# Cross-attention in fp32 on one core: the V·Wo and A products of two steps made back to back, with their 64-row parts side by side

## The chip, the cores and the metric

One core of a Trainium2 chip runs the whole program. The time is microseconds of device time for one execution, and the median of several runs is what counts. The kernel before takes 275.19 us, the median of three runs (275.04 to 275.63).

## The reference

Sixteen batches, each with 256 query rows of 256 features (`x`) and 77 context rows of 192 features (`ctx_768`), eight heads, all in fp32:

```
Q = x @ Wq ; K = c @ Wk ; V = c @ Wv           (8 heads of 256)
score = Q K^T / sqrt(256), masked where mask == 0
attn  = softmax(score)
out   = (attn @ V) @ Wo + x
out   = layernorm(out) * gamma + beta
```

## The kernel before

**Folded weights.** The kernel multiplies weights together first. `gA` and `gB` hold Wk·Wq^T per head, for the first 128 and the last 64 of the 192 context features; `uA` and `uB` hold Wv·Wo in the same way. A batch then needs A (context times g, which meets `x` directly in the scores) and VW (context times u, which meets the softmax weights directly in the output). Each of the two is a sum over 192 features, made as a product over 128 rows (part A) and one over 64 rows (part B) that accumulate in the same PSUM bank. In part B two products run at a time, one on rows 0 to 63 of TensorE and one on rows 64 to 127.

**Steps.** After the weights are folded (the first 52 us of the trace) a loop over `b` from -1 to 14 takes one batch per step. Step `b` makes the scores of batch `b + 1` (two tiles of 128 query rows, `scores`, L289), then VW of batch `b + 1` (`prepare_vw`, tiles `pv`, two banks, L214 for part A and L225 for part B) and a quarter of A for the next group of four batches (`prepare_a`, tiles `pa`, four banks, L172 and L186), and then the output product of batch `b`. For batches 0 to 10 that is `seven(b)` (L422, tiles `pm` and `po`): seven products of 2x2 blocks after Strassen's manner in place of eight. They need sums of softmax blocks, `sums(b)`, four POOL instructions at L402 to L405, and differences of VW blocks, `differences(b)`, L385 on POOL. Batches 11 to 15 use `attend` (L354). A for a group is needed only when its first batch is scored; the quarters for group g are spread over the four steps before, and steps with `b + 1` of 12 and more make none.

**The order on every engine is the order of the program**: no scheduler moves anything, and each engine does its instructions one after the other. The order in one step is:

- TensorE (PE): scores of both tiles; `pv` part A, `pa` part A, `pv` part B, `pa` part B; `seven(b)`.
- VectorE (DVE): `shift` of both tiles (bias and row maximum, L304 and L311), a transpose of `vr` in some steps (L279), then for each tile the layernorm statistics of an older batch and the sum and reciprocal of its own softmax (L324, L326); one `normalise`; the two transposes of the softmax weights (`turn`, L342); transposes of `x` in every second pair of steps (L150); one more `normalise`; two `add_product` (L469).
- ScalarE (ACT): eight exponentials for each tile (L318), two small activations for the layernorm (L498, L499), six copies out of PSUM (two of `pv`, four of `pa`, L926), the copy of `pm` to `m` (L445).
- GpSimd (POOL): the softmax weights `p` (L332, four instructions), `differences(b + 1)`, then `add_seven(b)`: two additions within `m` and three into the output rows (L455), then `sums(b + 1)`.
- The DMA queue of SyncE (SP) loads `x` and stores finished rows.

So `sums(b + 1)` stands behind `add_seven(b)` on POOL, and `add_seven(b)` needs the finished `seven(b)`, through `m` and through `add_product` on DVE. `seven` uses the sums in the order s2, s3, s1, s4, from its second product on; POOL makes them in the order s1, s3, s2, s4.

**PSUM** has eight banks, given out in turn by one pool, `ps_mm`. A step takes four for the scores, two for `pv`, four for `pa`, one for `pm` and one for `po`. A product that opens a bank waits until the bank's use eight allocations before has been read.

Of the kernel before, what the change touches and what calls it, by code (L numbers as in the profile page):

```python
# [8 lines left out]
F32 = mybir.dt.float32  # L9
# [6 lines left out]
P = 128  # L16
# [3 lines left out]
GB = 4  # L20
# [5 lines left out]
def kernel(  # L26
# [13 lines left out]
    nc = tc.nc  # L40
    B, S, DI = x.shape
# [3 lines left out]
    NG = B // GB  # L45
# [23 lines left out]
    ps_mm = ctx.enter_context(tc.tile_pool(name="ps_mm", bufs=8, space=PSUM))  # L69
# [36 lines left out]
    def flat(ap):  # L106
        return ap.rearrange("p a b -> p (a b)")

    def half(i):
        return slice(i * LB, (i + 1) * LB)  # L110
# [18 lines left out]
    def in_two(name, shape, g):  # L129
        return pools[g % 2].tile(shape, F32, tag=f"{name}{g % 2}", name=f"{name}_{g}", bufs=1)  # L130
# [19 lines left out]
        nc.vector.transpose(cols, cols)  # L150


    def prepare_a(g, places, B_first=False):


        if 0 in places:
            a_of[g] = in_two("a", [P, 2, GB, H, S2], g)
        parts = [
            (2 * u + i, dc) for u in places for dc in range(2) for i in range(2)
        ]  # L160
        batches = slice(g * GB, (g + 1) * GB)
        banks = []

        def cols(dc, i):
            return slice((2 * i + dc) * BK, (2 * i + dc + 1) * BK)

        def part_A():
            if not B_first:
                banks.extend(ring_of(parts))
            for (h, dc), o in zip(parts, banks):  # L170
                for i in range(NM):
                    nc.tensor.matmul(  # L172
                        flat(o[i * BK : (i + 1) * BK]),
                        gA[:, h, cols(dc, i)],
                        flat(cA[:, batches, :]),
                        start=not B_first,
                        stop=B_first,
                    )

        def part_B():  # L180
            if B_first:
                banks.extend(ring_of(parts))
            for j in range(0, len(parts), 2):
                for i in range(NM):
                    for k, (h, dc) in enumerate(parts[j : j + 2]):
                        nc.tensor.matmul(  # L186
                            flat(banks[j + k][i * BK : (i + 1) * BK]),
                            gB[half(k), h // 2, cols(dc, i)],
                            flat(cB[half(k), batches, :]),
                            start=B_first,  # L190
                            stop=not B_first,
                        )

        def ring_of(parts):
            return [
                ps_mm.tile([P, GB, S2], F32, tag="mm", name=f"pa_{g}_{h}_{dc}") for h, dc in parts
            ]

        def copies():
            return [(a_of[g][:, dc, :, h, :], o) for (h, dc), o in zip(parts, banks)]  # L200

        return part_A, part_B, copies

    def prepare_vw(b):

        vw_of[b] = vwp.tile([P, 4, 2, P], F32, tag="vw", name=f"vw_{b}", bufs=3)
        parts = slice(0, 4) if b < NS else slice(1, 5)
        pv = []

        def part_A():  # L210
            for k in range(2):
                pv.append(ps_mm.tile([P, 2 * DI], F32, tag="mm", name=f"pv_{b}_{k}"))
                for i in range(NM):
                    nc.tensor.matmul(  # L214
                        pv[k][i * BK : (i + 1) * BK],
                        cA[:, b, k * BK : (k + 1) * BK],
                        uA[:, parts, :, i],
                        start=True,
                        stop=False,
                    )  # L220

        def part_B():
            for i in range(NM):
                for k in range(2):
                    nc.tensor.matmul(  # L225
                        pv[k][i * BK : (i + 1) * BK],
                        cB[half(k), b, k * BK : (k + 1) * BK],
                        uB[half(k), parts, :, i],
                        start=False,
                        stop=True,  # L230
                    )

        def copies():
            return [
                (vw_of[b][:, :, k, :], pv[k].rearrange("p (q d) -> p q d", q=4)) for k in range(2)
            ]

        return part_A, part_B, copies

    def prepare_last():  # L240
# [35 lines left out]
    def turn_last(n):  # L276

        blocks = flat(vr[:, 2 * n : 2 * n + 2])
        nc.vector.transpose(blocks, blocks)  # L279
# [41 lines left out]
    def weigh(t):  # L321
        e = e_of.pop(t)
        den = st.tile([P, H], F32, tag="den", name=f"den_{t}")
        nc.vector.tensor_reduce(den, e, AX.X, ALU.add)  # L324
        rden = st.tile([P, H], F32, tag="rden", name=f"rden_{t}")
        nc.vector.reciprocal(rden, den)  # L326
        p = p_ring[t % 2]
        e_mh = e.rearrange("p (m h) k -> p m h k", h=2)
        rden_mh = rden.rearrange("p (m h) -> p m h", h=2)
        for cols, keys in ((slice(2 * KM), slice(KM)), (slice(2 * KM, 2 * S2), slice(KM, None))):  # L330
            part = p[:, :, cols].rearrange("p m (h k) -> p m h k", h=2)
            nc.gpsimd.tensor_tensor(  # L332
                part,
                e_mh[:, :, :, keys],
                rden_mh.unsqueeze(3).to_broadcast(list(part.shape)),
                ALU.mult,
            )
# [226 lines left out]
    with tc.tile_pool(name="wonce", bufs=1) as wp:  # L564
# [304 lines left out]
        for u in (uA, uB):  # L869
            t2, _, b22, b11, b12 = (u[:, q].rearrange("p n i c -> p (n i c)") for q in range(5))  # L870
# [12 lines left out]
    pools[1] = vwp = late  # L883


    assert QT == 2
    last = NT - 1
    for b in range(-1, B - 1):
        old = range(max(b - 1, 0) * QT, b * QT)
        now = range(max(b, 0) * QT, (b + 1) * QT)  # L890
        new = range((b + 1) * QT, (b + 2) * QT)
        for t in new:
            scores(t)
        if b == B - 2:
            for t in old:
                finish(t)
            spread(old[0], old[-1] + 1)
            invert(old[0], old[-1] + 1, aside=old)
            for t in old:
                normalise(t, aside=True)  # L900
        for t in new:
            shift(t)
        for n in range(0, 2) if b < 0 else range(b + 2, min(b + 3, B // 2)):
            turn_last(n)
        g, n = (b + 1) // GB + 1, (b + 1) % GB
        work = [prepare_vw(b + 1)]
        if g < NG:
            work.append(prepare_a(g, (n,)))
        for part_A, _, _ in work:
            part_A()  # L910
        for _, part_B, _ in work:
            part_B()
        for i, t in enumerate(new):
            exponential(t)
            if old and b < B - 2:
                finish(old[i])
            weigh(t)
        if old and b < B - 2:
            spread(old[0], old[-1] + 1)
        if b < 0:  # L920
            bias_of(GB, B)
            for j in range(GT // 2, GT, 2):
                transpose_x(0, j)
        for _, _, copies in work:
            for dst, src in copies():
                nc.scalar.copy(dst, src)  # L926
        if b + 1 < NS:
            differences(b + 1)
        if b < NS:
            if now:  # L930
                seven(b)
            if old:
                invert(old[0], old[-1] + 1)
                normalise(old[0])
            for t in new:
                turn(t)
            if n >= NF - 2:
                for j in range((n - NF + 2) * GT // 2, (n - NF + 3) * GT // 2, 2):
                    transpose_x(g, j)
            if old:  # L940
                normalise(old[1])


            if n == NF - 1:
                load_x(g)
            elif n:
                load_xT(g, (n - 1) * GT // 2, n * GT // 2)
            if now:
                add_seven(b)
            if b + 1 < NS:  # L950
                sums(b + 1)
            continue
        for t in now:
            attend(t)
        if b < B - 2:
            invert(old[0], old[-1] + 1, aside=old[:1])
            normalise(old[0], aside=True)
            turn(new[0])
            normalise(old[1])
            turn(new[1])  # L960
            for t in now:
                add_product(t)
        else:
            turn(new[0])
            finish(now[0])
            spread(now[0], now[1])
            turn(new[1])
# [16 lines left out]
    rstd, _ = rstd_of.pop(t)  # L984
# [40 lines left out]
```

## Time and profile before

| | |
|---|---|
| median of three runs | 275.19 us |
| the profiled execution: its own time | 274.39 us |
| its span in the trace | 272.6 us |
| PE busy | 265.9 us |
| DVE busy | 211.7 us |
| POOL busy | 158.7 us |
| ACT busy | 136.2 us |
| granted TensorE clock over the span | 0.998 |
| step from 104.96 to 119.06 us | 14.10 us |
| the same for a step with `attend` (217.76 to 229.14 us) | 11.38 us |

Matmuls overlap, and their ends in the trace are modelled, so a busy PE isn't a PE at its peak; distances between starts say more than durations. The trace has two rows for each fp32 product, so that sixteen rows are eight products in the code. A step is timed here from its first score product to that of the next step. Idle time of an engine is listed with what ended it.

### The profile page before, as it was taken

How to read it: one execution, taken by the hardware profiler on the slowest of the kernel's cores; microseconds unless marked ns; L12 is line 12 of the kernel's file. 1: busy time of each engine (PE TensorE's matmuls, PEld its weight loads, DVE VectorE, ACT ScalarE, POOL GpSimd, SP SyncE). 2: the span in 40 equal slices, each digit the busy share in tenths (PEclk: the TensorE clock that was granted, in tenths of full speed). 3: DMA queues.
4: the chain of work that ended last, by engine and by line, in shares of the span. 5: the costliest groups of instructions: out<-in, count | busy, mean ns of one | idle time of the engine just before them, and what ended most of it. 6: DMA issues, size and time to landing. Idle time of an engine off the chain costs nothing.

```text
span 272.6 us, 13577 instructions
## 1 busy us (share of the span) xinstructions
PE 265.9 (98%) x6056; PEld 188.3 (69%) x6056; DVE 211.7 (78%) x414; ACT 136.2 (50%) x436; POOL 158.7 (58%) x217
## 2 busy tenths in 40 slices
PE   7999999999999999999999999999999999999992
PEld 6557587857595949494949595858687767584662
DVE  0555929589759898979798888878797978879875
ACT  3233324364828281818273746464645544827652
POOL 1000003719887878786878787777777537245754
PEclk9999999999999999999999999999999999999999
DMA  6999989920000403210231314101405060110102
GB/s 192 200 199 190 328 143 195 277 30 2 2 5 4 114 9 109 90 42 4 60 62 42 81 44 155 41 6 38 84 5 118 5 195 2 41 44 0 64 22 77
DMA packets 42458, 22.63 MB, mean 83 GB/s; under 512 B 23632, under 2 KB 41632, under 8 KB 42400
## 3 DMA queue, kind: packets, MB, share of 16 engines
q1 hardware_dynamic: 42400, 21.77, 34.1%
q8 instruction: 47, 0.77, 1.2%
q14 instruction: 11, 0.09, 0.1%
HBM read 17.57 MB, written 4.19 MB: 80 GB/s over the span
## 4 chain that ended last, share of the span: by engine, by line
PE 91%; DMA 5%; SPq 2%; DVE 1%; issue 0%; DVEq 0%
PE ps L289 25%; PE pa L172 11%; PE pv L214 10%; PE po L422 9%; PE pm L422 8%; PE po L354 7%; PE pv L225 6%; PE pa L186 5%; DMA wk_blk<-in_L_xattn_Wk_dram 5%; PE pu L723 3%; PE pr L248 2%; PE pgb L783 1%; PE pw L737 1%; PE pr L260 1%; SPq L582 1%; PE po L370 1%
## 5 line engine op out<-in xcount | busy, mean ns | idle before, releaser
L318 ACT ACTIVATE e<-s,top 128x77 f32<-128x77 f32 x256 | 67.1, 348 | 68.8 <-DVE top L311 68.8
L332 POOL TENSOR_TENSOR p<-e,rden 128x512 f32<-128x512 f32 x64 | 47.6, 765 | 43.3 <-DVE rden L326 28.1
L289 PE MATMUL ps<-a,xT 128*32 128x154 f32 x2048 | 70.0, 294 | 0.0
L289 PEld LDWEIGHTS ps<-a,xT 128*32 128x32 f32 x2048 | 66.1, 110 | 1.7 <-issue 0.8
L304 DVE TENSOR_TENSOR s<-ps,bias 128x308 f32<-128x308 f32 x64 | 30.1, 475 | 18.2 <-PE ps L289 18.2
L172 PE MATMUL pa<-cA,gA 128*32 128x308 f32 x512 | 36.0, 423 | 0.0
L172 PEld LDWEIGHTS pa<-cA,gA 128*32 128x32 f32 x512 | 16.3, 110 | 20.6 <-issue 7.9
L214 PE MATMUL pv<-uA,cA 128*32 128x512 f32 x256 | 30.4, 592 | 0.0
L455 POOL TENSOR_TENSOR xg<-xg,m 128x256 f32<-128x256 f32 x33 | 24.1, 732 | 10.6 <-DVE xg L469 8.8
L324 DVE TENSOR_REDUCE den<-e 128x8 f32<-128x616 f32 x32 | 24.8, 775 | 4.5 <-ACT e L318 4.4
L311 DVE TENSOR_REDUCE top<-s 128x8 f32<-128x616 f32 x32 | 25.4, 795 | 1.1
L342 DVE STREAM_TRANSPOSE pT<-p 128x640 f32<-128x640 f32 x32 | 25.2, 813 | 0.8 <-POOL p L332 0.8
L926 ACT COPY vw<-pv 128x512 f32<-128x512 f32 x32 | 17.1, 586 | 8.1 <-PE pv L225 8.1
L385 POOL TENSOR_TENSOR ts<-vw 128x768 f32<-128x768 f32 x11 | 20.2, 1839 | 0.0
L538 DVE SCALAR_TENSOR_TENSOR xg<-xg,rstd,bet 128x256 f32<-128x256 f32 x24 | 18.8, 782 | 1.8
L186 PE MATMUL pa<-cB,gB 64*32 64x308 f32 x512 | 19.8, 420 | 0.0
L600 POOL COPY cRA<-cA 128x208 f32<-128x208 f32 x1 | 0.4, 357 | 29.7 <-DVE cA L599 29.7
L186 PEld LDWEIGHTS pa<-cB,gB 64*32 64x32 f32 x512 | 9.5, 107 | 11.6 <-issue 8.1
L225 PE MATMUL pv<-uB,cB 64*32 64x512 f32 x256 | 17.4, 601 | 0.0
L354 PE MATMUL po<-vw,pT 128*32 128x256 f32 x288 | 17.3, 380 | 0.0
L926 ACT COPY a<-pa 128x308 f32<-128x308 f32 x48 | 16.8, 454 | 0.0
L469 DVE TENSOR_TENSOR xg<-po,xg 128x256 f32<-128x256 f32 x31 | 11.7, 414 | 5.2 <-PE po L422 4.6
(117 smaller groups left out, 400.5 us busy)
## 6 DMA issues: line engine op xcount, KB each, us to landing
xT<-in_x_dram SPq DMA_DIRECT2D x32, 128.0 KB, 4.4
xg<-in_x_dram SPq DMA_DIRECT2D x4, 1024.0 KB, 6.4
out_dram<-xg SPq DMA_DIRECT2D x11, 256.0 KB, 2.6
wo<-in_L_xattn_Wo_dram SPq DMA_DIRECT2D x4, 512.0 KB, 6.3
wq_blk<-in_L_xattn_Wq_dram SPq DMA_DIRECT2D x12, 128.0 KB, 4.5
wvT<-in_L_xattn_Wv_dram SPq DMA_DIRECT2D x16, 96.0 KB, 4.1
out_dram<-xg SPq DMA_DIRECT2D x10, 128.0 KB, 1.7
wk_blk<-in_L_xattn_Wk_dram SPq DMA_DIRECT2D x12, 96.0 KB, 4.4
```

The source lines that it names most:

```text
L172: nc.tensor.matmul(flat(o[i * BK : (i + 1) * BK]), gA[:, h, cols(dc, i)], flat(cA[:, batches, :]), start=not B_first, stop=B_first,)
L186: nc.tensor.matmul(flat(banks[j + k][i * BK : (i + 1) * BK]), gB[half(k), h // 2, cols(dc, i)], flat(cB[half(k), batches, :]), start=B_fir ...
L214: nc.tensor.matmul(pv[k][i * BK : (i + 1) * BK], cA[:, b, k * BK : (k + 1) * BK], uA[:, parts, :, i], start=True, stop=False,)
L225: nc.tensor.matmul(pv[k][i * BK : (i + 1) * BK], cB[half(k), b, k * BK : (k + 1) * BK], uB[half(k), parts, :, i], start=False, stop=True,)
L289: nc.tensor.matmul(ps[m // 2][i * BK : (i + 1) * BK, m % 2 * 2 * S2 : (m % 2 + 1) * 2 * S2], xT_of[g][:, j * NM + m, dc], flat(a_of[g][:, ...
L304: nc.vector.tensor_tensor(s[:, a * H // 2 : (a + 1) * H // 2], ps[a][:, : H // 2 * S2].rearrange("p (h k) -> p h k", k=S2), bias[:, b, :]. ...
L311: nc.vector.tensor_reduce(top, s, AX.X, ALU.max, negate=True)
L318: nc.scalar.activation(e[:, h], s[:, h], AF.Exp, bias=top[:, h : h + 1])
L332: nc.gpsimd.tensor_tensor(part, e_mh[:, :, :, keys], rden_mh.unsqueeze(3).to_broadcast(list(part.shape)), ALU.mult,)
L354: nc.tensor.matmul(po[i * BK : (i + 1) * BK], pT[:, n, i], vw_of[b][:, 2 - n // 2 * 2 : 4 - n // 2 * 2, n % 2, :] if n < NF else vr[:, b, ...
L422: nc.tensor.matmul(out[i * BK : (i + 1) * BK], weight[:, i], moving, start=(n == 0), stop=(n == len(terms) - 1),)
L926: nc.scalar.copy(dst, src)
```

## The change

`prepare_vw` and `prepare_a` can now make their part B first: the 64-row products open the banks (`start`) and the 128-row products close them (`stop`). The order of parts within a product is decided by `rest_first`.

The loop makes the work for batches `b + 1` and `b + 2` in one step, when `b + 1` is even and below 14, and none in the step after. The pairs of batches are (0, 1), (2, 3) up to (12, 13): seven pairs. Batches 14 and 15 are made each in its own step, as before. In a step with a pair, PE does part A and part B of batch `b + 1`, then part B and part A of batch `b + 2`, and then `seven(b)`. The step after it does scores and `seven` alone.

On ACT, the six copies for batch `b + 1` stand after the exponentials of the step's first tile and ahead of those of the second; the six for batch `b + 2` stand where the copies stood before. The order of instructions on DVE, POOL and the DMA queue is as it was.

```diff
-    def prepare_a(g, places, B_first=False):
+    def prepare_a(g, places, rest_first=False):
...
-                        start=not B_first,
-                        stop=B_first,
+                        start=not rest_first,
+                        stop=rest_first,
...
-    def prepare_vw(b):
+    def prepare_vw(b, rest_first=False):
...
-        pv = []
+        pv = [ps_mm.tile([P, 2 * DI], F32, tag="mm", name=f"pv_{b}_{k}") for k in range(2)]
...
-                        start=True,
-                        stop=False,
+                        start=not rest_first,
+                        stop=rest_first,
...
-                        start=False,
-                        stop=True,
+                        start=rest_first,
+                        stop=not rest_first,
...
+    def work_of(b, rest_first=False):
+        g, n = b // GB + 1, b % GB
+        work = [prepare_vw(b, rest_first)]
+        if g < NG:
+            work.append(prepare_a(g, (n,), rest_first))
+        return work
+
+    def copy_out(work):
+        for _, _, copies in work:
+            for dst, src in copies():
+                nc.scalar.copy(dst, src)
+
...
-        work = [prepare_vw(b + 1)]
-        if g < NG:
-            work.append(prepare_a(g, (n,)))
-        for part_A, _, _ in work:
+        works = work_of(b + 1) if b + 1 >= B - 2 or n % 2 == 0 else []
+        for part_A, _, _ in works:
             part_A()
-        for _, part_B, _ in work:
+        for _, part_B, _ in works:
             part_B()
         for i, t in enumerate(new):
             exponential(t)
             if old and b < B - 2:
                 finish(old[i])
             weigh(t)
+            if i == 0 and works and b + 1 < B - 2:
+                copy_out(works)
+                works = work_of(b + 2, rest_first=True)
+                for _, part_B, _ in works:
+                    part_B()
+                for part_A, _, _ in works:
+                    part_A()
...
-        for _, _, copies in work:
-            for dst, src in copies():
-                nc.scalar.copy(dst, src)
+        copy_out(works)
```

More of the change, by code (lines that the diff above doesn't have):

```diff
@@ L167, in part_A @@
         def part_A():
-            if not B_first:
+            if not rest_first:
                 banks.extend(ring_of(parts))
@@ L175, in part_A @@
                         flat(cA[:, batches, :]),
-                        start=not B_first,
-                        stop=B_first,
+                        start=not rest_first,
+                        stop=rest_first,
                     )
         def part_B():
-            if B_first:
+            if rest_first:
                 banks.extend(ring_of(parts))
@@ L189, in part_B @@
                             flat(cB[half(k), batches, :]),
-                            start=B_first,
-                            stop=not B_first,
+                            start=rest_first,
+                            stop=not rest_first,
                         )
@@ L202, in prepare_a @@
         return part_A, part_B, copies
-    def prepare_vw(b):
+    def prepare_vw(b, rest_first=False):
         vw_of[b] = vwp.tile([P, 4, 2, P], F32, tag="vw", name=f"vw_{b}", bufs=3)
         parts = slice(0, 4) if b < NS else slice(1, 5)
-        pv = []
+        pv = [ps_mm.tile([P, 2 * DI], F32, tag="mm", name=f"pv_{b}_{k}") for k in range(2)]
         def part_A():
             for k in range(2):
-                pv.append(ps_mm.tile([P, 2 * DI], F32, tag="mm", name=f"pv_{b}_{k}"))
                 for i in range(NM):
@@ L228, in part_B @@
                         uB[half(k), parts, :, i],
-                        start=False,
-                        stop=True,
+                        start=rest_first,
+                        stop=not rest_first,
                     )
```

## The prediction

> **What bounds the kernel now.** I read the page's busy times first, then the chain of waits, then the order in time of each engine in a step from the middle.
>
> The page, busy time by engine:
>
> ```profile
> PE 265.9 (98%) x6056; PEld 188.3 (69%) x6056; DVE 211.7 (78%) x414; ACT 136.2 (50%) x436; POOL 158.7 (58%) x217
> ```
>
> The chain of waits between 100 and 131 us (start, length, what), one full step:
>
> ```profile
> 105.15 4.19 PE ps L289 x128
> 109.33 1.72 PE pv L214 x16
> 111.05 2.07 PE pa L172 x32
> 113.12 1.02 PE pv L225 x16
> 114.14 1.04 PE pa L186 x32
> 115.18 1.89 PE pm L422 x64
> 117.06 2.18 PE po L422 x80
> 119.25 4.19 PE ps L289 x128
> ```
>
> Nothing but PE stands in it, so PE never waits for another engine inside a step. Everything else has slack only as long as it is ready when PE gets there, and that is what a new order on PE can break. The order in time of that step, for those who feed PE:
>
> ```profile
> 112.91 3.08 POOL L332 TENSOR_TENSOR p<-e,rden 128x512 f32<-128x512 f32 x4 [1.83 <-ACT e L318]
> 115.11 0.65 PE L422 MATMUL pm<-vw,pT 128*32 128x128 f32 x16
> 115.95 1.84 POOL L385 TENSOR_TENSOR ts<-vw 128x768 f32<-128x768 f32 x1
> 117.18 0.59 ACT L445 COPY m<-pm 128x512 f32<-128x512 f32 x1 [0.59 <-PE pm L422]
> 119.06 4.37 PE L289 MATMUL ps<-a,xT 128*32 128x154 f32 x128
> 119.82 2.35 POOL L455 TENSOR_TENSOR xg<-xg,m 128x256 f32<-128x256 f32 x3 [0.83 <-DVE xg L469]
> 122.13 0.73 POOL L402 TENSOR_TENSOR ss<-pT 128x256 f32<-128x256 f32 x1
> 123.62 0.73 POOL L404 TENSOR_TENSOR ss<-pT,ss 128x256 f32<-128x256 f32 x1
> ```
>
> Here `seven` starts at 115.11 and the next scores at 119.06, 3.95 us later. The sum s2 (L404), which the second product of the next `seven` needs, ends at 124.35, which is 5.29 us after those scores began. Before, ten microseconds of other products (4.19 + 1.72 + 2.07 + 1.02 + 1.04) lie between the start of the scores and that `seven`.
>
> **The change, part by part.** S is the start of a step's first score product.
>
> *Fewer changes between 128-row and 64-row products (gain).* In the chain, products over 128 rows take equal time for equal columns: the 80 rows of `po`, 128 columns each, take 2.18 us, so the 64 of `pm` should take 64/80 of it, 1.74; they take 1.89, 0.15 more, and they come right behind 64-row products. The 32 rows of `pa` part B, 308 columns each, take 1.04, so 16 rows of 512 columns should take 0.86; `pv` part B takes 1.02, 0.16 more, right behind 128-row products. A pair of changes costs 0.31. Before, two steps have two pairs; after, one. Seven times 0.31 is 2.2 us gained. The bounds: nothing, if B behind B' (marked ' is the work for batch b + 2) costs a change too, and 7 x 0.35, if the pipeline restarts a little more often than I see. I take 2.1. The Trainium skill, "TensorEngine Tiling (Array Packing)", Key Properties, says that a change of tiling mode drains TensorE, while another tile of the same mode doesn't; that rule alone would let the change be faster, by the sum just given.
>
> *Part B' must find its banks free.* Counting banks, the four banks of `pa'` are those of `pv` and the first two of `pa`, so B' waits for the copies on ACT, which the change puts behind the first tile's exponentials. By the middle step, exponentials of the first tile run from S + 3.75 to 5.85, `pv` part B ends so that the copies start at S + 9.27, take 1.07 for `pv` (to 10.34) and 1.40 for all `pa` (the second of these ends at about 10.95). PE would get to the first pair of `pa'` at 10.9 and to the second at 11.4. No wait if ACT is on time. Where the short step before leaves DVE behind, it isn't: I work out below that this happens once or twice, for 0.4 in all (bounds 0 and 2).
>
> *PE of the long step.* Up to the end of part B it is as before, S + 10.0. B' adds 0.86 + 1.04, a change 0.15, A' 1.72 + 2.07; `seven(b)` starts at T = S + 15.85, the next scores at T + 3.95.
>
> *The second tile's exponentials* now stand behind six copies on ACT: they start at S + 11.75 in place of 5.85 and end at 13.85. Row sum and reciprocal on DVE (0.76 + 0.20) give 14.95, the weights on POOL (1.54) 16.6, `differences` (1.84) 18.45. The two additions within `m` come next and their input `m` is ready at T + 2.66, that is S + 18.5. So POOL is just in time, and the delay of 5.9 us costs nothing as long as A' covers it; with a dearer chain each tenth is a tenth on the sums. Behind the wait on DVE stand `normalise`, `turn`, the transposes of x in every second pair (1.26) and `add_product`. With the transposes DVE gets to `add_product` at S + 20.25, 0.2 after `seven` is done; without, it is on time.
>
> *The short step (loss).* There scores run straight into `seven(b + 1)`. PE gets to its second product at 4.19 + 0.46 = 4.65 us behind the start of scores. s2 stands behind `add_seven(b)` on POOL, which starts as before with `add_product` after `seven(b)`, and so still ends 5.29 us behind the start of scores. The wait is 0.64, plus the time from POOL's end to PE's start. No row of before shows PE waiting for POOL; the nearest are POOL to DVE (`p` to its transpose, 0.03) and PE to ACT (0.3); I take 0.15. So PE stands idle 0.8 us in steps 2, 4, 6, 8, 10, and 0.2 more in the three behind transposes: 4.6 us. The other inputs, `differences`, VW and the softmax transposes, are there earlier. s4, needed 1.9 us behind s2, ends 0.8 behind it.
>
> *The first short step (b = 0)* has no `add_seven` ahead, but its sums wait for the late exponentials. These lines are step -1 in the order of time:
>
> ```profile
> 61.76 1.08 ACT L926 COPY vw<-pv 128x512 f32<-128x512 f32 x2 [1.38 <-PE pv L225]
> 64.16 1.74 POOL L560 TENSOR_TENSOR bias<-bias,nan 128x924 f32<-128x924 f32 x1
> 65.85 1.83 POOL L385 TENSOR_TENSOR ts<-vw 128x768 f32<-128x768 f32 x1
> 69.14 0.74 POOL L404 TENSOR_TENSOR ss<-pT,ss 128x256 f32<-128x256 f32 x1
> ```
>
> Copies until 64.12, exponentials until 66.2, row sum and reciprocal until 67.25, then the bias of the later batches on DVE (0.70 + 1.12, to 69.1), the small POOL steps and the bias on POOL as in these lines (63.58 to 65.90 there; 69.5 to 71.85 now), `differences` next, and s2 ends 4.03 behind the start of `differences`, at 75.85. PE: part B ends where step 0 began, 62.64; less one change 62.5; with B', A' and a change 68.35; scores to 72.55; the first product to 73.0. The wait ends at 76.0: 3.0 us lost (2.4 to 3.4).
>
> *No cost:* the moved copies and exponentials are as many as before. No DMA, DVE or POOL instruction is moved. DVE (12 us of work in a step) falls 3 to 4 us behind in a short step of 9 us and makes it up in the long one, 20 us; this is what delays the first exponentials of a long step from S + 5.85 to about S + 8.6, with both transposes of x and of `vr` (1.26 more) to about 9.9. The copies then start 0.6 late, and B', with 0.2 to 0.4 to spare, waits for the rest: this is the 0.4, which takes two such places. The last pair, batches 12 and 13, is followed by `attend`, which takes no sums: its transposes are ready at about S + 13.7 and needed at S + 17.8.
>
> *Sum:* -2.1 + 0.4 + 4.6 + 3.0 = +5.9 us. Against the profiled execution (274.39, span 272.6) that is 280.3, and against the median, 0.8 above it, 281.1.
>
> The first wait, 3.0 us, is the longest that PE would have behind the first score product; the granted clock of before is 1.00 in the steps that I read up to 251.89 us, and no row there tells what such a wait does to it. The Trainium skill, "TensorE: Matmul & The Clock Gate", Why this matters for your kernels, asks for no PE gap above some 3 us, or the clock falls to half; at that rule's window of about 3.4 us at half speed, an estimate from that page, the sum would be some 1.7 us higher.
>
> **Rivals.**
>
> *The sums are in time (faster, other side).* If s2 ended 0.8 us sooner relative to `seven`, the five waits would go and only the changes count. It decides at 5.29 against 4.65 us. POOL has no idle time between `add_seven` and L404, and 0.83 ahead of it is the wait for PE and DVE, which the change doesn't shorten: against. With the first step's wait gone as well it would be 275.2 - 2.1 = 273.1. Chance 0.06.
>
> *Banks bind.* If ACT comes 1 us later than I think in most long steps, because DVE starts the shift late, B' waits each time, and so does the chain behind the second exponentials: 0.6 on PE in each of six long steps, 3.6, and as much again at the sums if POOL, which is just in time, slips with it; less the 0.4 that I have, 287.9 at most and 284.5 with the first alone. DVE's 78% speaks for it, the 0.4 to 3.4 us of slack against. Chance 0.12.
>
> *The change doesn't do what it says:* the 0.31 stays, because opening a bank or the neighbouring B costs as much. Then 283.2. The 64-row `pa` behind `pv` shows no such cost. Chance 0.10.
>
> *Half the waits,* if POOL is faster with DVE held elsewhere: 278.3. Chance 0.10; the forecast itself has 0.62.
>
> **How the numbers follow.** 0.2% is about what a measurement of this kernel can tell from no change (0.55 us). Only the first rival ends below: faster 0.06, within 0.2% 0.02 (the case of half the waits, at its end, cancels the gain), slower 0.92. The forecast's own bounds are 2.4 + 5 x 0.6 - 2.4 = +3.0 and 3.4 + 5 x 1.2 + 1 - 1.5 = +8.9; from 278.2 to 284.1. This leaves out the first rival and the end of the second.
>
> **What would show it.** The chain of waits has POOL `ss` in it (L403 in the new numbering), and PE waits some 0.8 to 1.0 us for it in five short steps and about 3 us in the first; short steps take about 9 us and long ones 19.8, against 2 x 14.10. The long step has one pair of changes. The granted clock stays at 1.00. I am wrong if PE doesn't wait at all in short steps, if the waits lie in the long steps at `pa'`, or if the pair of changes isn't cheaper.

## The result, and the profile after

The changed kernel takes 282.04 us, the median of five runs (281.67 to 282.60); the kernel before took 275.19 beside it. The ratio is 1.0248, with an interval of 1.0224 to 1.0272: slower by 2.5%, 0.9 us above the forecast and inside its range. The execution shown took 282.13 us, its span is 280.3, 7.7 more than the 272.6 of before (by the medians the difference is 6.85; the execution of before that the profile shows was 0.8 us quicker than its median). Line numbers from here on are those of the changed kernel: from `prepare_vw` to `add_product` they are one lower than before (scores L288, `pm` and `po` L421, sums L401 to L404).

The busy time by engine, and further down the page the chain that ended last:

```profile
PE 266.5 (95%) x6056; PEld 190.6 (68%) x6056; DVE 209.9 (75%) x414; ACT 134.0 (48%) x436; POOL 157.6 (56%) x217
...
PE 58%; DVE 13%; ACT 10%; POOL 10%; DMA 5%; SPq 2%; issue 2%; DVEq 0%; POOLq 0%; ACTq 0%
```

PE has the same work to do (6056 rows, 266.5 us of modelled busy time against 265.9) in a longer span. Before, 91% of the chain was PE; now a third of it is DVE, ACT and POOL. What PE waits for now and didn't before (us in total, times, the longest):

```profile
PE pm L421 <- POOL ss L403: 4.8, 6, 2.1
PE po L353 <- DVE pT L341: 1.4, 1, 1.4
```

The first row is the sum s2, six times. The second, transposed softmax weights in the last step, is in no sum of the forecast. The chain through one wait for s2:

```profile
95.32 1.75 PE pm L421 x64
97.07 2.23 PE po L421 x80
99.29 0.02 issue
99.32 0.44 DVE xg L468
99.75 0.07 issue
99.82 0.74 POOL xg L454
...
101.44 0.73 POOL xg L454
102.18 0.69 POOL ss L401
102.87 0.70 POOL ss L402
103.57 0.07 issue
103.64 0.74 POOL ss L403
104.38 0.04 issue
104.42 1.52 PE pm L421 x48
105.94 2.18 PE po L421 x80
```

From the end of `seven` at 99.3 us the chain leaves PE for `add_product`, three additions and three sums, and comes back at 104.42. On PE the next scores lie beside that and end sooner:

```profile
99.07 4.37 PE L288 MATMUL ps<-a,xT 128*32 128x154 f32 x128
103.25 0.62 PE L421 MATMUL pm<-vw,pT 128*32 128x128 f32 x16
104.42 0.65 PE L421 MATMUL pm<-vw,ss 128*32 128x128 f32 x16 [0.55 <-POOL ss L403]
```

The first product at 103.25 and the second at 104.42 are 1.17 us apart where 0.43 to 0.46 is usual, so the wait costs 0.73 (0.55 by the row, the rest while the weights are loaded behind it).

The time by step, as stretches from one step's first scores to the next's (length; busy us and rows of PE, PEld (TensorE's weight loads), DVE, ACT, POOL; granted clock; DMA share; GB/s):

```profile
53.00:68.88 15.88, 15.88 (x322) 8.94 (x324) 8.26 (x16) 8.79 (x28) 2.83 (x4) 1.00 0.25 35
68.88:79.28 10.40, 8.33 (x276) 8.05 (x272) 9.26 (x17) 5.15 (x19) 8.97 (x13) 1.00 0.01 3
79.28:99.07 19.79, 19.79 (x473) 12.84 (x469) 13.39 (x27) 9.82 (x31) 14.56 (x19) 1.00 0.02 4
99.07:107.94 8.87, 8.32 (x281) 8.03 (x276) 7.31 (x17) 4.69 (x19) 5.97 (x8) 1.00 0.40 92
107.94:128.16 20.22, 20.22 (x473) 12.92 (x467) 17.23 (x33) 10.01 (x33) 15.50 (x21) 1.00 0.24 68
...
223.19:280.30 57.11, 49.94 (x1088) 33.25 (x1079) 47.74 (x106) 28.38 (x96) 29.23 (x43) 0.99 0.17 53
```

The last stretch, from the scores of batch 12 on, in the kernel before:

```profile
217.76:272.60 54.84, 50.04 (x1088) 32.86 (x1080) 43.38 (x98) 28.68 (x96) 26.73 (x39) 0.99 0.18 55
```

PE has as much to do in it, but DVE brings 4.4 us of work more into it (47.74 against 43.38). The 7.7 us of the span, part by part:

| part | before | after | difference |
|---|---|---|---|
| up to the first scores (loads) | 52.47 | 53.00 | +0.53 |
| steps -1 and 0 | 24.29 | 26.28 | +1.99 |
| steps 1 to 10, five pairs | 141.00 | 143.91 | +2.91 |
| from the scores of batch 12 | 54.84 | 57.11 | +2.27 |

A short step takes 8.11 us where nothing waits (two of the experiments below show it), so the first wait costs 10.40 - 8.11 = 2.29 and the other five 0.76 each. A long step takes 19.79 where no bank waits, so a pair without waits takes 27.90 against 28.20: 0.30 is saved.

### The profile page after: what moved, and what is told of

It is laid out like the page before. It is cut to its first block, busy times and chain, and to the rows that moved or that the text cites. A ratio compares the mean times of both kernels' runs of the same rounds, so it can differ in the third digit from the quotient of the medians.

```text
span 280.3 us, 13587 instructions
## 1 busy us (share of the span) xinstructions
PE 266.5 (95%) x6056; PEld 190.6 (68%) x6056; DVE 209.9 (75%) x414; ACT 134.0 (48%) x436; POOL 157.6 (56%) x217
## 4 chain that ended last, share of the span: by engine, by line
PE 58%; DVE 13%; ACT 10%; POOL 10%; DMA 5%; SPq 2%; issue 2%; DVEq 0%; POOLq 0%; ACTq 0%
PE ps L288 10%; PE pa L172 10%; ACT e L317 8%; PE po L421 8%; PE pv L213 7%; PE pm L421 6%; PE pa L186 5%; DMA wk_blk<-in_L_xattn_Wk_dram 5%; PE pv L224 4%; POOL xg L454 3%; PE pu L722 3%; DVE pT L341 2%; PE pr L247 2%; DVE xg L468 2%; DVE den L323 2%
## 5 line engine op out<-in xcount | busy, mean ns | idle before, releaser
L288 PE MATMUL ps<-a,xT 128*32 128x154 f32 x2048 | 69.9, 294 | 0.0
L288 PEld LDWEIGHTS ps<-a,xT 128*32 128x32 f32 x2048 | 66.3, 110 | 1.4 <-issue 0.3
L303 DVE TENSOR_TENSOR s<-ps,bias 128x308 f32<-128x308 f32 x64 | 28.4, 469 | 7.9 <-PE ps L288 7.9
L895 ACT COPY a<-pa 128x308 f32<-128x308 f32 x48 | 17.4, 438 | 0.6
L213 PEld LDWEIGHTS pv<-uA,cA 128*32 128x32 f32 x256 | 7.6, 110 | 13.4 <-issue 12.5
```

Of the source, the lines that this page charges most:

```text
L213: nc.tensor.matmul(pv[k][i * BK : (i + 1) * BK], cA[:, b, k * BK : (k + 1) * BK], uA[:, parts, :, i], start=not rest_first, stop=rest_first,)
L288: nc.tensor.matmul(ps[m // 2][i * BK : (i + 1) * BK, m % 2 * 2 * S2 : (m % 2 + 1) * 2 * S2], xT_of[g][:, j * NM + m, dc], flat(a_of[g][:, ...
L303: nc.vector.tensor_tensor(s[:, a * H // 2 : (a + 1) * H // 2], ps[a][:, : H // 2 * S2].rearrange("p (h k) -> p h k", k=S2), bias[:, b, :]. ...
```

## The experiments

The theory at first: the loss is PE's waits for s2, the first of them made by the bias work on POOL. The rivals: the dearer part is at the end, where DVE or the missing cover of a product delays `attend`; and the price of the changes between 128-row and 64-row products isn't what I took.

**The last pair undone.** Only the last pair, batches 12 and 13, goes back to two single steps.

```diff
-        works = work_of(b + 1) if b + 1 >= B - 2 or n % 2 == 0 else []
+        works = work_of(b + 1) if b + 1 >= B - 4 or n % 2 == 0 else []
...
-            if i == 0 and works and b + 1 < B - 2:
+            if i == 0 and works and b + 1 < B - 4:
```

> The changed kernel with batches 12 and 13 made each in its own step again; the pairs (0, 1) to (10, 11) stay. In the changed kernel the stretch from the scores of batch 12 to the end takes 57.1 us against 54.8 before, 2.3 us more where I had forecast 0.3 less. Theory A, the last pair's own short step keeps DVE and ACT late until the end: with full steps of 11.4 us for 9.7 us of DVE work the lag of some 4.5 us is worked off by the last step, the stretch takes about 54.8, the time is 279.8 (279.4 to 280.2) and no wait for the transposed softmax is left. Theory B, the lag handed on by the short step before (batch 11) is enough: the stretch stays near 57 us and the time at 282.0 or, without the gain of one pair, 282.3.

It took 281.18 us (280.77 to 283.44), ratio 1.0249 (1.0204 to 1.0293). The wait for `pT` is gone, and the stretch from the scores of batch 12 takes 56.17 us (223.03 to 279.2): 0.94 of the 2.27 are gone, 1.33 stay. (The times alone wouldn't show it: the ratio is that of the kernel after, 1.0248.) So the last pair explains less than half of what the end lost, and each of the two theories named there has its half.

**Two pairs undone.** The same with `B - 6` in both conditions: pairs only up to (8, 9).

> The changed kernel with the pairs (0, 1) to (8, 9) alone; batches 10 to 13 are made each in its own step. The run with batches 12 and 13 apart took only half of the 2.3 us off the end (56.2 us from the scores of batch 12 on, before 54.8): DVE came 3.9 us late out of the short step ahead and was still 1.6 us late in the last step. If that lag is the cause, two more full steps work it off: the stretch from the scores of batch 12 takes 54.8, and the time is 2.3 + 0.5 us under the changed kernel, 279.3 (278.8 to 279.7). If the end is long for another reason: 281 or more.

280.54 us (279.69 to 282.51), ratio 1.0212 (1.0178 to 1.0246), 1.2 us above what the theory gave; the profiled execution lost 1.65 us in step 0 to the clock, of which more below. The stretch from the scores of batch 12:

```profile
225.89:280.70 54.81, 50.03 (x1088) 32.84 (x1079) 44.76 (x101) 28.57 (x96) 26.71 (x39) 0.99 0.18 55
```

That is the 54.84 of before: with two ordinary steps of 14.10 us between the last short step and the end, nothing is lost there. The reason is DVE's lag. ACT's first exponentials of batch 12, in the kernel before and after:

```profile
221.51 4.20 ACT L318 ACTIVATE e<-s,top 128x77 f32<-128x77 f32 x16 [5.04 <-DVE top L311]
...
230.78 2.11 ACT L317 ACTIVATE e<-s,top 128x77 f32<-128x77 f32 x8 [7.62 <-DVE top L310]
```

The scores began at 217.76 and 223.19, and ACT stood idle for DVE's row maximum. The time from a step's first scores to its first exponential, in us (3.75 in the steps before, without lag 4.1 in the last one, where layernorm work stands ahead):

| batch scored | 12 | 13 | 14 | 15 |
|---|---|---|---|---|
| before | 3.75 | 3.69 | 3.68 | 4.09 |
| after | 7.59 | 4.87 | 6.64 | 6.93 |
| last pair undone | 7.60 | 6.50 | 5.39 | 5.68 |
| two pairs undone | 4.24 | 3.68 | 3.69 | 4.08 |

A short step of 8.87 us is shorter than DVE's work (11.9 to 12.5 us in the steps of 14.10 before), and what DVE owes then is paid off at about 1.1 us for each step of 11.38 us up to batch 14 (7.60, 6.50, 5.39). The rate isn't PE's 11.38 less DVE's 9.7 us of work: DVE and ACT wait for each other in turn (row maximum, exponentials, row sum), and that chain takes 10.27 us for a batch (first exponentials at 230.63, 240.90 and 251.17 in the run with the last pair undone). Into batch 15, where layernorm work stands ahead of the exponentials, it takes 11.67 (to 262.84), and nothing more is paid off. In the kernel after, the steps of batches 12 and 13 make 13.95 + 8.50 = 22.45 us instead of 2 x 11.38, so they don't pay it off either. At batch 15 the exponentials are 2.84 us late (6.93 - 4.09), and the last step is 2.57 longer (23.28 us from its first scores to the end, before 20.71); the pair saves 0.31 of it elsewhere. The chain of the kernel after at that place:

```profile
252.28 4.11 ACT e L317 x16
256.41 0.81 DVE den L323
257.45 0.71 DVE pT L341
...
262.95 1.09 ACT xg L531 x2
264.04 4.01 ACT e L317 x16
268.07 0.81 DVE den L323
269.10 0.71 DVE pT L341
270.16 0.44 DVE bn L476
```

There is no PE in it. From the scores of batch 12 to the end the chain is on DVE and ACT, but for some 2.3 us on POOL.

**The sums ahead of `add_seven` on POOL.**

```diff
-            if now:
-                add_seven(b)
             if b + 1 < NS:
                 sums(b + 1)
+            if now:
+                add_seven(b)
```

> The changed kernel with the four POOL instructions of sums(b + 1) placed ahead of the five of add_seven(b). My theory: PE's 0.74 us waits in the five short steps hang on add_seven standing ahead of the sums; they go (3.7 us), the 2.1 us wait in step 0 stays, since no add_seven stands there. As each short step is then 0.74 us shorter and DVE has as much to do, DVE comes later into the long steps, and part is given back as waits for PSUM banks there, 1.5 to 2.5 us: 280 to 281. If nothing is given back, 278.3. Rival, another input of seven is as late as the sums: 282.0, and the trace names that input.

282.13 us (281.42 to 284.49), ratio 1.0282 (1.0233 to 1.0330): no gain, a miss. PE's waits show where it went:

```profile
PE po L353 <- DVE pT L341: 2.1, 1, 2.1
PE pm L421 <- POOL ss L403: 2.1, 1, 2.1
...
PE pa L172 <- DVE xg L468: 1.3, 2, 0.7
```

Five of the six waits for s2 are gone and the short steps take 8.11 us. But then DVE has still less time in them, and long steps take 21.11, 20.37, 20.87 and 20.13 where 19.79 is free of waits. In the two longest `pa` waits for a bank that `add_product` reads, and in all four weight loads of B' wait for ACT's copies (0.28 to 0.41 us). The five pairs lose 1.84 instead of 2.91, and the end (57.9) 0.8 more than after. So the wait for s2 is real, but under it lies DVE, and most of what POOL gives back is lost again behind it.

The same edit in the kernel before, as a control:

> The kernel before with the four POOL instructions of sums(b + 1) ahead of the five of add_seven(b), as a control for the order on POOL: PE never waits for either there, so 275.0, no change (within 0.4 us).

274.92 us (274.18 to 275.79), ratio 0.9999 (0.9985 to 1.0012). With the cover of ten microseconds of products, the order of POOL is free.

**The price of a change of rows, from both sides.** In the changed kernel the pair is made as A, B, A', B', so that B' no longer stands beside B:

```diff
-                works = work_of(b + 2, rest_first=True)
-                for _, part_B, _ in works:
-                    part_B()
+                works = work_of(b + 2)
                 for part_A, _, _ in works:
                     part_A()
+                for _, part_B, _ in works:
+                    part_B()
```

> The changed kernel with part A of the second batch of a pair made ahead of its part B, so that the order on PE is A, B, A', B', seven: two more changes between 128-row and 64-row products for each of the seven pairs, nothing else. My theory, a pair of changes costs 0.31 us: 7 x 0.31 = 2.2 us, 284.2 (283.7 to 284.5), if each lands on the path. Rival, the order of parts is worth nothing: 282.0.

283.30 us (282.62 to 284.74), ratio 1.0316 (1.0280 to 1.0352), 1.3 above the changed kernel by the medians and 1.9 by the ratios, where the theory gave 2.2. A long step without a bank wait takes 20.08 against 19.79, so 0.29; where a bank wait of up to 0.4 lay in it, it takes 20.21 against 20.22: the later B' has its bank free. That gives back 0.5 in two steps, and another 0.27 and 0.26 come back from shorter waits in step 0 and at the end. And in the kernel before, `pv` and `pa` each do A and then B:

```diff
-        for part_A, _, _ in work:
+        for part_A, part_B, _ in work:
             part_A()
-        for _, part_B, _ in work:
             part_B()
```

> The kernel before, with the parts in the order pv A, pv B, pa A, pa B in place of pv A, pa A, pv B, pa B: one more pair of changes between 128-row and 64-row products in each of the twelve steps that make both; the amount of work is the same. By the price read from the chain of waits, 12 x 0.31 = 3.7 us: 278.9. If the excess of 0.15 and 0.16 us belongs to the bank or the stage and not to the change of rows: 275.2.

278.74 us (277.93 to 278.87), ratio 1.0145 (1.0123 to 1.0166). Twelve steps have one pair of changes more, 3.9 us: 0.325 for a pair by the times, 0.30 by a step (106.10 to 120.50 is 14.40 against 14.10). The price of 0.31 stands. The Trainium skill, "TensorEngine Tiling (Array Packing)", Key Properties, says that a change of mode drains TensorE; these two runs agree with it and put a size on it here.

**The bias of the later batches made later.** The call goes from step -1 to the end of step 0.

```diff
         if b < 0:
-            bias_of(GB, B)
             for j in range(GT // 2, GT, 2):
...
+            if b == 0:
+                bias_of(GB, B)
```

> The changed kernel with the bias of the later batches (two instructions on DVE, four on POOL, 2.3 us) made at the end of step 0 in place of step -1, so that nothing stands between the softmax weights and the differences and sums of batch 0. My theory of the first wait (2.1 us measured, 3.0 forecast): the sums end some 2 us earlier and the wait falls to 0.4 or less: 280.1 (279.8 to 280.5), and no run has the stretch at reduced clock that one profile showed behind this wait. Rival, the wait is for the late exponentials alone, with the bias beside them: 282.0.

279.65 us (279.43 to 280.20), ratio 1.0173 (1.0149 to 1.0196), 2.1 us less than after by the ratios, 2.4 by the medians. Step 0 takes 8.11 us in place of 10.40, and of the six waits for s2 five short ones are left:

```profile
PE pm L421 <- POOL ss L403: 2.9, 5, 0.8
```

The first wait is the bias work on DVE and POOL, as forecast.

**A longer first wait.** The addition of the bias is made twice on the later batches (it adds zeros, so nothing changes), to see whether the clock follows a wait.

```diff
-        nc.gpsimd.tensor_tensor(part, part, nan.to_broadcast([P, hi - lo, S2]), ALU.add)
+        for _ in range(1 + (lo > 0)):
+            nc.gpsimd.tensor_tensor(part, part, nan.to_broadcast([P, hi - lo, S2]), ALU.add)
```

> The changed kernel with the addition of the bias (L560 of the kernel before, 1.74 us on POOL) made twice in step -1; it adds zeros, so the values stay. PE's wait in step 0 grows from 2.1 (2.3 with the weight load) to about 3.8 us. Two profiles had, behind the wait of 2.1 us, a stretch of 3.4 us at half clock, the others none. Theory, the clock falls when a wait covers a whole window of its monitor: with 3.8 us it falls in every run, and the time is 282.0 + 1.7 + 1.7 = 285.4. Rival, the clock has nothing to do with the wait: 283.7 with the clock as before.

286.20 us (285.45 to 288.76), ratio 1.0401 (1.0344 to 1.0459). PE's rows around the wait:

```profile
72.66 0.62 PE L421 MATMUL pm<-vw,pT 128*32 128x128 f32 x16
77.12 1.08 PE L421 MATMUL pm<-vw,ss 128*32 128x128 f32 x16 [3.84 <-POOL ss L403]
77.98 1.93 PE L421 MATMUL pm<-ts,ss 128*32 128x128 f32 x32
```

And the stretches of the same execution, with the granted clock third from the end:

```profile
75.00:79.00 4.00, 1.88 (x36) 1.76 (x40) 2.38 (x5) 2.39 (x10) 3.84 (x6) 0.61 0.00 0
79.00:83.37 4.37, 4.37 (x101) 4.09 (x96) 1.69 (x2) 0.59 (x1) 4.19 (x6) 0.57 0.02 4
83.37:90.00 6.63, 6.63 (x164) 4.69 (x160) 5.05 (x10) 2.11 (x8) 5.06 (x7) 1.00 0.01 2
```

From the end of the wait to the next scores it takes 6.25 us where the kernel after takes 3.52: the wait of 3.84 costs 2.7 us more than itself. The clock fell before the wait was over: it was 0.50 from 76 us on, and the wait ends at 77.12. Only this execution has a trace, but all four take 285.45 us or more, where the wait alone would have given 283.7. In the kernel after, with 2.07 us (2.3 with the weight load), the clock stayed at 1.00 (the second stretch of its table), and so it did at 2.08 with the last pair undone. But in the profiled execution of the kernel with the sums ahead, a wait of 2.06 was enough:

```profile
75.00:81.95 6.95, 5.18 (x128) 5.18 (x132) 4.99 (x9) 4.42 (x17) 5.66 (x9) 0.75 0.01 2
```

Its step 0 took 12.05 us in place of 10.40, 1.65 lost, and so did that of the kernel with two pairs undone (12.04, a wait of 2.04). The Trainium skill, "TensorE: Matmul & The Clock Gate", Why this matters for your kernels, puts the bound at an idle gap of some 3 us; the 3.84 agree with that. At 2.04 to 2.08 us the clock fell in two profiled executions and not in two others, which that bound doesn't foresee; what decides it there isn't shown.

**Fewer pairs, further apart.** Pairs only in steps -1, 2, 5 and 8, with ordinary steps between them; the sums first on POOL where a pair was made; `add_product` early in the short steps; the later bias at the end of step 1.

```diff
+    pairs = (0, 3, 6, 9)
...
-        works = work_of(b + 1) if b + 1 >= B - 2 or n % 2 == 0 else []
+        works = work_of(b + 1) if b not in pairs else []
...
+            if b in pairs:
+                for t in now:
+                    add_product(t)
...
+            if b + 1 in pairs:
+                sums(b + 1)
```

> A version from what the runs show: pairs only in steps -1, 2, 5 and 8 (batches 0 and 1, 3 and 4, 6 and 7, 9 and 10), so that behind each short step there stands at least one full step of 14.1 us; the sums ahead of add_seven in the long steps; add_product of a short step ahead of its normalise; the bias of the later batches at the end of step 1. Theory: the loss is the work of DVE and POOL, 12 us in every step, which a short step of 8 us can't take; with a full step to catch up only the gain of the row changes is left, 4 x 0.3 = 1.2 us, less 0.4 for what is left of the first wait: 0.4 to 1.2 us under the kernel before, 274.0 to 274.6. Rival, the waits come back at the banks of the step behind: 275.5 or more.

277.60 us (276.48 to 278.05), ratio 1.0085 (1.0064 to 1.0107): the theory missed by 3 us, and it is the rival's case. The waits for s2 are gone (short steps 8.12), the long steps take 19.79, but two of the ordinary steps behind a short one take 15.06 in place of 14.10, where `pa` waits for a bank that DVE's shift reads (1.5 us in all by the rows, 1.9 by the steps), and batch 11's step takes 12.01 in place of 11.38. One short step took 9.95, with PE standing for 1.5 us on nothing that the profile shows.

**A lighter DVE in the short steps.** The same, with both `normalise` and the transposes of `x` of a short step put off to the next:

```diff
+            if b in pairs:
+                late_of.append((g, n, old))
+            else:
+                turn_x(g, n)
```

> The version with spaced pairs (steps -1, 2, 5 and 8), which came out at 277.6 us, with one thing more: a short step makes neither its two normalise nor its transposes of x; the step behind it does them, after its own transposes of the softmax weights. In the version before this, DVE still had 6 us of these to do when the scores of the next step began, and PE waited 0.8 us, twice, at the third bank of A for the bias additions. Theory, these bank waits are DVE's lag: they go (1.9 us over the two steps of 15.07), and 275.7 is left with the 1.5 us pause in step 3, which the profile puts down to nothing; without that pause 274.2. Rival, the lag only moves one step on: 277 or more.

278.84 us, the median of eight runs (276.17 to 281.38). The longest lies 1.9% above the quickest and isn't in the ratio, 1.0088 (1.0054 to 1.0123); without it the median is 278.74. PE's waits for banks that DVE reads are gone as expected, but the kernel isn't faster. PE's waits inside the steps are now only such pauses (the others are from the start of the program):

```profile
PE ps L288 <- issue: 1.7, 2, 1.0
...
PE po L421 <- issue: 0.8, 1, 0.8
```

**The load of `x` in quarters.** Two of these three pauses, and the one of the kernel ahead, came during or behind a load of 1 MB of `x`, so I split that into four of 256 KB, one in each step:

```diff
-            if n == NF - 1:
-                load_x(g)
-            elif n:
+            load_x_part(g, n)
+            if 0 < n < NF - 1:
```

> The kernel with four spaced pairs and lighter short steps (e9, 278.84 us), with the load of x split into four of 256 KB, one in each step, in place of one of 1 MB in every fourth step. Theory L (the pauses of PE in which it waits for nothing that the profile shows come from the 1 MB load beside them): the pauses at about 120.7 and 165.3 us, 0.81 and 0.96 us, go; the one at 221.6 us (0.77 us), with no load beside it, is left; 276.5 to 277.3 us, a ratio of about 1.001 to 1.005. Theory N (the load has nothing to do with it): pauses of 0.7 to 1.5 us stay somewhere in the steps, and the time stays at 278 to 279 us, a ratio of about 1.009.

> The kernel with four spaced pairs (e7, 277.6 us, ratio 1.0085), with the load of x split into four of 256 KB, one in each step. Theory L: the pause of 1.5 us at 117.93 us goes (that step 8.4 to 8.5 us in place of 9.95), and with it the time falls to about 276.1 us, a ratio of about 1.003. Theory N: a pause of 0.7 to 1.5 us stays, at that place or another, and the ratio stays at 1.007 to 1.010.

277.62 us (276.52 to 278.93), ratio 1.0077 (1.0047 to 1.0106), and 277.42 (276.13 to 279.76), ratio 1.0084 (1.0055 to 1.0112): no clear gain over the ratios of 1.0088 and 1.0085 with the load in one. In the first of the two the pauses moved:

```profile
62.30 2.23 PE L178 MATMUL pa<-cA,gA 128*32 128x308 f32 x26 [2.09 <-issue]
210.37 1.90 PE L294 MATMUL ps<-a,xT 128*32 128x154 f32 x51 [0.83 <-issue]
```

In the second the profiled execution (276.82) has only one, of 0.15 us, while others of the same kernel took up to 279.76. So the 1 MB load isn't needed for the pauses. Late instructions are a rival that no run tests: in the queue that the page calls `instruction`, a packet lies 0.6 to 2.1 us ahead of each of the six pauses, but 47 such packets pass in every one of these executions, before and after too. What makes the pauses, and why the kernels with spaced pairs have them where before and after show none inside the loop, stays open. No version beat the kernel before.

## Why the prediction was right

The forecast of +5.9 us stands against +6.85 by the medians and +7.7 in the span that the parts are read from; 0.5 of the 7.7 is the loads ahead of the loop, which the change doesn't touch. Step by step:

- *Fewer changes of rows, -2.1.* Right: seven pairs at 0.30 are 2.1, and two experiments bought the same change back at 0.29 and 0.325. The rival that the change doesn't do what it says is out.
- *Banks for B', 0.4, in one or two places.* Right: two long steps took 20.22 and 19.98 in place of 19.79, 0.6 in all. The rival that banks bind in most long steps is out.
- *Five short waits, 4.6.* Right in kind and place, somewhat large: 0.76 each, 3.8 in all. The 0.2 that I added behind the transposes of `x` didn't come: all five short steps take about 8.87. PE was back some 0.04 us after POOL; with 0.2 more for the weights it is nearly the 0.15 that I took between the two. (One row of before does show PE waiting for POOL, for `ident` at the start of the program, with 0.06 us between the two.) Both rivals with earlier sums are out.
- *The first wait, 3.0 (2.4 to 3.4).* Right mechanism, shown by moving the bias (step 0 is 2.3 shorter); the size is 2.3, a little under my lower bound: I had DVE's bias work 0.2 us too long and POOL's start behind it 0.3 us too late. The wait ended 6.9 us behind the start of the scores (68.88 to 75.76) where I had 7.65 (68.35 to 76.0).
- *No cost of the last pair.* This step failed, and it is the largest error. I asked when the transposes of batch 13 are ready in their own step, and for that they were in time. What I left out is where DVE's lag ends up. I had put it at 3 to 4 us for a short step, rightly (3.84 at batch 12), and written that DVE "makes it up in the long one, 20 us". Behind step 10 there is no step of 20 us any more: there are the last pair's 13.95 and 8.50, in which the lag only shrinks from 3.84 to 2.96, and one step of 11.38, in which it stays (2.84 at batch 15). What DVE owes reaches the last tile, where nothing can hide it: +2.57 in the last step. The two runs that undo the last pairs show it, by 0.94 and then by all of it.
- *The clock stays at 1.00.* So it did in the profiled execution. But the wait of some 2.1 us lies where the clock fell in other executions, of two sibling kernels.
- *The rivals' numbers.* Two don't come out of their own terms: banks that bind, without the slip at the sums, give 281.1 - 0.4 + 3.6 = 284.3, not 284.5, and half of all the waits off 281.1 leaves 277.3, not 278.3. Nothing else hangs on them.

The two errors, waits 1.5 us too dear and an end 2.6 us too cheap, partly hid each other: that the total came out so near is in part luck.

## What to carry to other kernels

An engine at 75 to 78% whose lag is "made up later" has to be followed to the last tile: find the first stretch behind the change that is too short to pay the lag off. When work is moved out of every second step, the emptied step waits for its slowest chain, here POOL's sums; with those out of the way, what DVE owes comes up in the steps behind. A gain of 0.3 us on PE couldn't carry that. And a wait taken away is worth only the distance to the next one under it: 3.8 us of waits removed gave 1.1 in the pairs and took 0.8 at the end.

## What the runs showed of the hardware

The granted clock of TensorE can fall behind a pause of 2.04 to 2.08 us: to 0.75 over the 7 us that hold the wait, in two profiled executions and not in two others of nearly the same program, at a cost of 1.65 us. In a pause of 3.84 us it fell in the one profiled execution, at a cost of 2.7 us beyond the pause.

PE can stand for 0.8 to 2.1 us on nothing that the profile shows, in the kernels with spaced pairs. In the one with `x` in quarters the longest:

```profile
58.00:60.00 2.00, 2.00 (x22) 0.51 (x15) 1.91 (x4) 1.41 (x6) 0.00 (x0) 1.00 0.90 137
60.00:62.30 2.30, 0.21 (x3) 0.00 (x0) 1.45 (x3) 0.00 (x0) 0.67 (x1) 1.00 0.12 19
```

The DMA engines were busy for 0.90 ahead of it and nearly idle within it. In the pause that ends at 221.59 us of the kernel with lighter short steps there is no transfer at all. The cause wasn't found.
